# Transposed attention weights in tiles of four heads, one piece per row, two tiles in turn

## The chip, the cores and the metric

The kernel runs on one NeuronCore of a Trainium2 chip. The metric is the device time of one execution in microseconds (us); lower is better. The engines named below are TensorE (PE, matrix products; PEld is its weight load), VectorE (DVE), ScalarE (ACT), GpSimd (POOL) and SyncE (SP), which only issues transfers here. The memories are SBUF, of 128 partitions, PSUM, into which TensorE writes, and the chip's main memory.

## What is computed

One transformer layer on 32 sequences of 100 tokens with 256 features, in float32. A normalized `x` attends to a context of 361 tokens with 16 heads of 64 features; the result is added to `x`. Then comes a feed-forward part with weights and activations rounded to 8 bits, which the change doesn't touch.

```
xn = layernorm(x)                                   # 32 x 100 x 256
Qh, Kh, Vh = xn@WQ, ctx@WK, ctx@WV                  # 16 heads of 64
logits = Qh @ Kh^T / 8 + mask * -1e9                # per head 100 x 361
attn = softmax(logits)
x = x + concat(attn @ Vh) @ WO
x = x + ffn_8bit(layernorm(x))
```

## The kernel before, in words

The 32 sequences ("batches") are worked off one after the other, in groups of four. The first and the last are cut in three parts; the 30 between are "whole" and run through `whole_batch` (L800). For TensorE, VectorE, ScalarE and GpSimd the order of the instructions in that stretch is the order of the Python code; only SP's order is chosen by a scheduler.

A whole batch does its 16 heads in two halves of eight. For each half, TensorE multiplies queries by keys (`products`, L451), one head per PSUM bank. VectorE adds the mask and takes the minimum of each row (`minima`, L465), writing the logits to `pb`, which holds eight heads. ScalarE takes the exponential (L479). TensorE meanwhile makes the keys of the next batch (`k_part`, L285). VectorE divides by the row sums (`divide`, L487 and L494), four heads at a time.

The product with V needs the weights transposed, context tokens on the partitions. The query rows of a head stand in four blocks of 32 partitions, 25 tokens in each. `blocks` (L522) is a VectorE instruction per head that transposes every 32 x 32 block in its place, into the tile `xT`. In it, partition block k still belongs to query block k. `send` (L527) moves the blocks to where they belong with 16 transfers from SBUF to SBUF (L533), issued by SP: for each of four source blocks of 32 partitions and four destination blocks, 32 rows of three pieces (one for each of the three chunks of 128 context tokens) of 200 numbers (eight heads of 25 tokens). There is one `xT` tile for eight heads, with one buffer (`NX` is 1), and one `pT` tile, the destination, for each half.

`attend` (L561) multiplies V by the transposed weights on TensorE. It runs for the batch before: all of batch i-1 stands in TensorE's order after the first half's keys of batch i, and before the second half's `products`. It reads a head's weights from `pT` as four runs of 25 numbers.

After the second half come `residuals`, V of the batch itself (`v_part`, L316; three of its copies on VectorE and three on ScalarE, L324), and once per group of four the queries (`q_part`, L378) and the output projection (`project_T`, L598). SP also issues one load of context per batch (L215), for the batch after the next two; it waits until TensorE has finished with the buffer.

The order around the change, in `whole_batch`:

```
for q in range(half * NQ // 2, (half + 1) * NQ // 2):
    divide(i, range(2 * PAIRS * q, 2 * PAIRS * (q + 1)))
    blocks(i, range(2 * PAIRS * q, 2 * PAIRS * (q + 1)))
send(i, half)
if half == 0:
    attend(i - 1)
```

Of the kernel before, what the change touches and what calls it, by code (L numbers as in the profile page):

```python
# [8 lines left out]
F32 = mybir.dt.float32  # L9
# [18 lines left out]
def kernel(  # L28
# [16 lines left out]
    P = 128  # L45
# [6 lines left out]
    NHP = E // P  # L52
    NFC = F // P
    NSC = 3
    SC = P
    SP = NSC * SC
# [3 lines left out]
    PAIRS = 2  # L60
    NQ = NHP // PAIRS
    HP = NHP // 2
# [5 lines left out]
    QB = 32  # L68
    NQB = P // QB
    TB = T // NQB  # L70
# [97 lines left out]
    with ExitStack() as att:  # L168
        wpool = att.enter_context(tc.tile_pool(name="wpool", bufs=1))
        p1 = att.enter_context(tc.tile_pool(name="p1", bufs=1))  # L170
# [20 lines left out]
        NB = 4 * PAIRS  # L191
        pb = wpool.tile([P, NB, SP], F32, tag="p", name="p")
# [16 lines left out]
        def bank(name):  # L209
            return psum.tile([P, 512], F32, tag="ps", name=name)  # L210
# [28 lines left out]
        for k in range(2):  # L239
            nc.scalar.dma_start(  # L240
                out=maskh[k * RH : k * RH + TH], in_=mask[k * TH : (k + 1) * TH]
            )
        for k in range(NQB):
            nc.scalar.dma_start(
                out=maskt[k * QB : k * QB + TB], in_=mask[k * TB : (k + 1) * TB]
# [18 lines left out]
        steps = []  # L264
# [4 lines left out]
        def whole(i):  # L269
            return steps[i][2] == NHP  # L270
# [131 lines left out]

        pTs, aTs, wides = {}, {}, {}

        def wide(i, half):

            b = steps[i][0]
            if (b, half) not in wides:
                wides[b, half] = p1.tile(
                    [SC, NSC * NQB, NHP * TB], F32, tag=f"pT{half}", name=f"pT{b}_{half}"  # L410
                )
            return wides[b, half]

        def weights_T(i, pair, on_vector):

            h0 = 2 * pair
            pts = [bank(f"pt{i}_{pair}_{k}") for k in range(2)]
            for h in range(2):  # L420
                for c in range(NSC):
                    for k in range(2):
                        ks = slice(k * RH, k * RH + TH)
                        nc.tensor.transpose(
                            pts[k][:SC, (h * NSC + c) * TH : (h * NSC + c + 1) * TH],
                            pb[ks, (h0 + h) % NB, c * SC : (c + 1) * SC],
                            ident[ks, ks],
                        )
            n = 2 * NSC * T
            pT = pTs[i, pair] = wide(i, pair // HP).rearrange("s c t -> s (c t)")[  # L430
                :, pair % HP * n : (pair % HP + 1) * n
            ].rearrange("s (c t) -> s c t", t=T)
            copies = []
            for k in range(2):
                src = pts[k][:SC, : 2 * NSC * TH].rearrange("p (c t) -> p c t", t=TH)
                copy = nc.vector.tensor_copy if k == 0 and on_vector else nc.scalar.copy
                copies.append(copy(pT[:, :, k * TH : (k + 1) * TH], src))
            return copies
# [69 lines left out]

        xTs, NX = {}, 1

        def blocks(i, heads):


            half = heads[0] // NHP
            if (i, half) not in xTs:
                xTs[i, half] = p1.tile(
                    [P, SP // QB, NHP * TB + QB - TB], F32, tag="xT", name=f"xT{i}_{half}", bufs=NX
                )  # L520
            for h in heads:
                nc.vector.transpose(  # L522
                    xTs[i, half][:, :, h % NHP * TB : h % NHP * TB + QB],
                    pb[:, h % NB, :].rearrange("t (c s) -> t c s", s=QB),
                )

        def send(i, half):  # L527

            src = xTs[i, half].rearrange("p (c m) t -> p c m t", c=NSC)
            dst = wide(i, half).rearrange("s (c k) t -> s c k t", c=NSC)  # L530
            for m in range(P // QB):
                for k in range(NQB):
                    nc.sync.dma_start(  # L533
                        out=dst[m * QB : (m + 1) * QB, :, k, :],
                        in_=src[k * QB : (k + 1) * QB, :, m, : NHP * TB],
                    )

        def attend(i, pairs=None):


            b, first, n = steps[i]
            if pairs is not None:
                first, n = pairs
            g, j = b // G, b % G

            def weights(pair, k, c):
                if not whole(i):
                    return pTs[i, pair][:, k * NSC + c, :]
                h = 2 * (pair % HP) + k
                return wide(i, pair // HP)[:, c * NQB : (c + 1) * NQB, h * TB : (h + 1) * TB]  # L550

            if first == 0 and j == 0:
                aTs[g] = p1.tile([P, NHP, G, T], F32, tag="aT", name=f"aT{g}")
            for p0 in range(first, first + n, HP):
                m = min(HP, n)
                av = bank(f"av{i}_{p0}")
                for pair in range(p0, p0 + m):
                    for c in range(NSC):
                        for k in range(2):
                            h = 2 * (pair % HP) + k  # L560
                            nc.tensor.matmul(  # L561
                                av[k * DK : (k + 1) * DK, (pair - p0) * T : (pair - p0 + 1) * T],
                                vs[b, pair // HP][:, c, h * DK : (h + 1) * DK],
                                weights(pair, k, c),
                                start=(c == 0),
                                stop=(c == NSC - 1),
                            )
                copied = nc.scalar.copy(  # L568
                    aTs[g][:, p0 : p0 + m, j, :],
                    av[:, : m * T].rearrange("p (c t) -> p c t", t=T),  # L570
                )
            return copied
# [227 lines left out]
        def whole_batch(i):  # L800

            b = steps[i][0]
            g, j = b // G, b % G
            if not whole(i - 1):
                for pair in range(steps[i - 1][1], steps[i - 1][1] + steps[i - 1][2]):
                    weights_T(i - 1, pair, True)
            if b - 1 + NCB < B:
                load_ctx(b - 1 + NCB)  # L810
            for half in range(2):
                heads = range(half * NHP, (half + 1) * NHP)
                minima(i, products(i, range(half * HP, (half + 1) * HP)))
                n = steps[i + 1][2] // 2
                keys = range(half * n, (half + 1) * n)
                exponentials(i, heads[:6])
                for pair in keys[: n // 2]:
                    k_part(i + 1, pair)
                exponentials(i, heads[6:])
                for pair in keys[n // 2 :]:  # L820
                    k_part(i + 1, pair)
                for q in range(half * NQ // 2, (half + 1) * NQ // 2):
                    divide(i, range(2 * PAIRS * q, 2 * PAIRS * (q + 1)))
                    blocks(i, range(2 * PAIRS * q, 2 * PAIRS * (q + 1)))
                send(i, half)
                if half == 0:
                    attend(i - 1)
            residuals(i, range(2), None)
            if j == G - 2:
                ln1_T(g + 1)  # L830
            v_part(b, 0, 0)
            for piece in todo.pop(0) if todo else ():
                piece()
            for c in range(1, NSC):
                v_part(b, 0, c)
            while later:
                normalize(later.pop(), None)
            for c in range(NSC):
                v_part(b, 1, c)
            if j == G - 3:  # L840
                ln1(g + 1)
            group_work(i, range(2))
            if g == NG - 1 and j >= 1:
                project(b - 1, range(NHP))
# [11 lines left out]
        i = len(steps) - 1  # L856
# [23 lines left out]
    h = hpool.tile([P, NFC, N], F32, tag="h", name="h")  # L880
# [132 lines left out]
    k = 0  # L1013
# [3 lines left out]
    src = xg[0].rearrange("t b d -> t (b d)")  # L1017
# [20 lines left out]
    for u, (g, n) in enumerate(units):  # L1038
# [3 lines left out]
        for fc in range(NFC):  # L1042
# [4 lines left out]
            m = GT // cut  # L1047
            for part in range(cut):
# [16 lines left out]
                if fc + 1 in ends and (u, fc - 1) not in paired:  # L1065
                    src = h[:, fc + 1 - spans[ends.index(fc + 1)] : fc + 1, at if cut > 1 else ts]
# [12 lines left out]
            if (u, fc) in rounded:  # L1079
                i = rounded[u, fc]  # L1080
# [7 lines left out]
            if (u, fc) in ((3, 0), (3, 3)):  # L1088
                p = (2, 4) if fc == 0 else (2, 6)
# [15 lines left out]
    with tc.high_priority():  # L1105
        rh, hih, c2, _, _, found, bounds, product = affine_params(ext2, "h", scales["2"][1])
# [7 lines left out]
    def part(i):  # L1114

        return 2 if blocks[i][1] < 3 or i == len(blocks) - 3 else G
# [18 lines left out]
    for i, (first, n) in enumerate(blocks):  # L1135
# [3 lines left out]
        for k in range(2):  # L1139
            sl = slice(k * NF2, (k + 1) * NF2)  # L1140
            t = f2.tile([P, NF2, G * P], I16, tag=f"ih{k}", name=f"ih{i}_{k}")[:, :, : n * P]
# [16 lines left out]
        m = part(i)  # L1158
# [59 lines left out]
```

## Time and profile before

| what | value |
|---|---|
| median of three runs | 1374.21 us (1372.69 to 1375.06) |
| the profiled execution | 1374.26 us |
| its span, first to last instruction | 1372.5 us |
| PE busy | 1283.0 us (93%) |
| DVE busy | 956.2 us (70%) |
| ACT busy | 583.1 us (42%) |
| mean granted TensorE clock | 0.966 |
| bytes moved by DMA | 106.66 MB, mean 78 GB/s |
| transfers of `send` | 960, of 75.0 KB each, in pieces of 800 bytes |

The span is the time from the first to the last instruction of the profiled execution; the time of the whole execution is 1.8 us longer. Busy time counts computing instructions. The issue of a transfer is not counted as busy; it is listed with the queue that issues it, "SPq" for SP, and its duration is the time that the queue is taken by it. "Landing" is when a transfer's completion is known. An arrow in a wait names what the instruction waited for.

### The profile page before, as it was taken

What the parts mean: (1) busy time and instruction counts of PE and PEld (TensorE: products, weight loads), DVE (VectorE), ACT (ScalarE), POOL (GpSimd) and SP (SyncE); (2) the same over time, 40 slices, a digit from 0 to 9 for tenths busy, and PEclk for the clock granted to TensorE, in tenths of its full rate; (3) what the DMA queues carried; (4) which work ended last, traced back from release to release, by engine and by line L of the source; (5) the groups of instructions that cost most, each with busy time, mean ns of one, the idle gap of its engine ahead of it and who ended that gap; (6) DMA issues with size and microseconds to landing.
All of it is one profiled execution on the core that took longest, in us unless ns stands there. A gap on an engine that the chain in (4) does not pass through costs nothing.

```text
span 1372.5 us, 21080 instructions
## 1 busy us (share of the span) xinstructions
PE 1283.0 (93%) x7186; PEld 743.6 (54%) x7188; DVE 956.2 (70%) x2803; ACT 583.1 (42%) x1570; POOL 111.3 (8%) x195
## 2 busy tenths in 40 slices
PE   9999899889999899899998999899998999998858
PEld 4645556555555565455555555455564555555526
DVE  4666675876577676776757775776668775775798
ACT  2544244433344443342444434344443333442685
POOL 1000000110010100110001100110001100102250
PEclk9999999899998999899998999899999999999998
DMA  8143323323322432333223323323332333221112
GB/s 237 35 109 77 75 59 81 76 72 78 83 69 58 120 75 61 85 85 76 66 66 86 77 68 80 89 63 79 68 77 73 77 83 83 57 62 46 49 54 96
DMA packets 132507, 106.66 MB, mean 78 GB/s; under 512 B 17224, under 2 KB 130448, under 8 KB 132400
## 3 DMA queue, kind: packets, MB, share of 16 engines
q1 hardware_dynamic: 129312, 98.60, 29.6%
q0 software_dynamic: 2144, 5.38, 1.4%
q10 hardware_dynamic: 944, 1.34, 0.3%
q8 instruction: 57, 0.93, 0.3%
q14 instruction: 50, 0.41, 0.1%
HBM read 24.97 MB, written 6.55 MB: 23 GB/s over the span
## 4 chain that ended last, share of the span: by engine, by line
PE 51%; DVE 18%; SPq 17%; DMA 5%; issue 4%; POOL 2%; ACT 2%; DVEq 0%; POOLq 0%
SPq L533 17%; PE pv L316 13%; PE pk L285 12%; DVE xT L522 10%; PE pq L378 6%; PE py L598 5%; DMA pT<-xT 5%; PE av L561 5%; PE sc L451 5%; DVE p L494 3%; PE pf L1164 2%; ACT h L1060 1%; DVE p L465 1%; DVE st L626 1%; POOL r L987 1%
## 5 line engine op out<-in xcount | busy, mean ns | idle before, releaser
L522 DVE STREAM_TRANSPOSE xT<-p 128x384 f32<-128x384 f32 x480 | 277.3, 578 | 238.3 <-DMA pT<-xT 226.0
L479 ACT ACTIVATE p<-p,m 128x361 f32<-128x361 f32 (+1 forms) x512 | 299.0, 587 | 258.4 <-DVE m L465 258.2
L285 PE MATMUL pk<-c,wkt 128*128 128x361 f32 x1016 | 345.1, 495 | 36.1 <-DVE m L465 36.0
L316 PE MATMUL pv<-wvt,c 128*128 128x512 f32 x768 | 336.1, 593 | 0.0
L285 PEld LDWEIGHTS pk<-c,wkt 128*128 128x128 f32 x1016 | 198.3, 200 | 182.5 <-DVE m L465 73.0
L465 DVE CUSTOM_DVE_ANT_0 p<-sc,maskt 128x361 f32<-128x361 f32 x480 | 222.4, 529 | 76.2 <-PE sc L451 76.1
L316 PEld LDWEIGHTS pv<-wvt,c 128*128 128x128 f32 x768 | 144.3, 190 | 170.6 <-issue 166.7
L451 PE MATMUL sc<-kT,q 64*128 64x361 f32 (+1 forms) x1024 | 207.0, 494 | 15.8 <-DVE v L324 7.4
L494 DVE TENSOR_SCALAR p<-p,r 128x361 f32<-128x361 f32 (+1 forms) x512 | 174.6, 405 | 4.4
L324 ACT COPY v<-pv 128x512 f32<-128x512 f32 x90 | 52.8, 586 | 251.5 <-PE pv L316 251.5
L451 PEld LDWEIGHTS sc<-kT,q 64*128 64x128 f32 (+1 forms) x1024 | 102.4, 188 | 103.3 <-DVE v L324 23.3
L561 PE MATMUL av<-pT,v 128*64 128x100 f32 x3072 | 144.9, 252 | 11.2 <-DMA pT<-xT 5.3
L561 PEld LDWEIGHTS av<-pT,v 128*64 128x64 f32 x3072 | 136.2, 137 | 31.0 <-issue 16.2
L292 ACT COPY kT<-pk 128x361 f32<-128x361 f32 x254 | 111.6, 451 | 61.5 <-PE pk L285 61.4
L479 ACT ACTIVATION_READ_ACCUMULATOR p<-p,m 128x1 f32 (+1 forms) x512 | 96.0, 187 | 0.0
L645 POOL TENSOR_SCALAR v<-mv 100x1 f32<-100x1 f32 x31 | 8.4, 272 | 1053.9 <-DVE mv L627 1053.6
L378 PE MATMUL pq<-xnT,wqt 128*128 128x400 f32 x256 | 87.9, 500 | 0.2 <-ACT xnT L369 0.2
L568 ACT COPY aT<-av 128x400 f32<-128x400 f32 (+2 forms) x67 | 31.9, 476 | 107.8 <-PE av L561 107.8
L598 PE MATMUL py<-aT,wot 128*128 128x400 f32 x224 | 76.4, 499 | 0.0
L324 DVE COPY v<-pv 128x512 f32<-128x512 f32 x102 | 65.0, 676 | 9.9 <-PE pv L316 9.8
L378 PEld LDWEIGHTS pq<-xnT,wqt 128*128 128x128 f32 x256 | 48.4, 190 | 38.8 <-issue 3.3
L598 PEld LDWEIGHTS py<-aT,wot 128*128 128x128 f32 x224 | 42.6, 190 | 34.0 <-issue 3.4
(148 smaller groups left out, 692.1 us busy)
## 6 DMA issues: line engine op xcount, KB each, us to landing
pT<-xT SPq DMA_DIRECT2D x960, 75.0 KB
c<-in_ctxT_dram SPq DMA_DIRECT2D x31, 361.0 KB
x<-in_x_dram SPq DMA_DIRECT2D x8, 400.0 KB
xb<-xb POOLq DMA_DIRECT2D x32, 100.0 KB, 2.5
x<-xb SPq DMA_DIRECT2D x5, 384.0 KB
out_dram<-x SPq DMA_DIRECT2D x5, 256.0 KB
out_dram<-x SPq DMA_DIRECT2D x3, 384.0 KB
wqt<-in_wq_dram SPq DMA_DIRECT2D x4, 256.0 KB
```

Source lines behind the costliest of these rows:

```text
L285: nc.tensor.matmul(pk[:, :S], wkt[q][:, dc, col * P : (col + 1) * P], c[:, dc, :S], start=(dc == 0), stop=(dc == NDC - 1),)
L316: nc.tensor.matmul(pv[:SC, :], c[:, dc, s * SC : (s + 1) * SC], wvt[h][:, dc, :], start=(dc == 0), stop=(dc == NDC - 1),)
L324: return copy(vs[b, h][:, s, :], pv[:SC, :])
L378: nc.tensor.matmul(pq[:, :GT], wqt[q][:, dc, pair * P : (pair + 1) * P], xnTs[g][:, dc, :], start=(dc == 0), stop=(dc == NDC - 1),)
L451: nc.tensor.matmul(pss[h], qbuf[pair // PAIRS][k * DK : (k + 1) * DK, pair % PAIRS, b % G, :n], kT[k * DK : (k + 1) * DK, pair, :], start= ...
L465: done = nc.vector.tensor_tensor_reduce(pb[:n, h % NB, :S], ps, maskh if halved(steps[i][0]) else maskt, 1.0, BIG, ALU.add, ALU.min, ms[h] ...
L479: nc.scalar.activation(s, s, AF.Exp, bias=ms[h][:n], scale=-1.0, accum_out=sums[i][0][:n, h : h + 1])
L494: nc.vector.tensor_scalar(s, s, r[:n, h : h + 1], None, ALU.mult)
L522: nc.vector.transpose(xTs[i, half][:, :, h % NHP * TB : h % NHP * TB + QB], pb[:, h % NB, :].rearrange("t (c s) -> t c s", s=QB),)
L533: nc.sync.dma_start(out=dst[m * QB : (m + 1) * QB, :, k, :], in_=src[k * QB : (k + 1) * QB, :, m, : NHP * TB],)
L561: nc.tensor.matmul(av[k * DK : (k + 1) * DK, (pair - p0) * T : (pair - p0 + 1) * T], vs[b, pair // HP][:, c, h * DK : (h + 1) * DK], weigh ...
L598: nc.tensor.matmul(py[:, :GT], wot[:, c, dc * P : (dc + 1) * P], aT[:, c, :, :].rearrange("p j t -> p (j t)"), start=(c == 0), stop=(c == ...
```

## The change

The transposed weights of four heads now have a tile of their own, and two such `xT` tiles are used in turn (`NX` is 2, `NH` is 4 heads). There are four `pT` tiles for a batch, one for each four heads. In both tiles the three chunks of a row stand one behind the other: `RUN` is 4 x 25 + 7 = 107 numbers, of which the last 7 are what a 32-wide block writes beyond its 25, so that a row of one source and one destination block is one piece of 3 x 107 = 321 numbers, 1,284 bytes. `send` is called behind each four heads, with 16 transfers each time, of 32 rows of one piece; in the order of SP's instructions a batch now has 64 of them in place of 32. `blocks` writes its 12 blocks by chunk and destination block, in four dimensions. `attend` reads the same four runs of 25 numbers at other distances, and the parts of the first and last batch that don't use `send` keep their copies in the same, now smaller, tiles.

```
+        NH = 2 * PAIRS
+        RUN = NH * TB + QB - TB
-        def wide(i, half):
+        def wide(i, pair):
-            b = steps[i][0]
-            if (b, half) not in wides:
-                wides[b, half] = p1.tile(
-                    [SC, NSC * NQB, NHP * TB], F32, tag=f"pT{half}", name=f"pT{b}_{half}"
+            b, g = steps[i][0], 2 * pair // NH
+            if (b, g) not in wides:
+                wides[b, g] = p1.tile(
+                    [SC, NQB, NSC * RUN], F32, tag=f"pT{g}", name=f"pT{b}_{g}"
                 )
...
-        xTs, NX = {}, 1
+        xTs, NX = {}, 2
...
-            half = heads[0] // NHP
-            if (i, half) not in xTs:
-                xTs[i, half] = p1.tile(
-                    [P, SP // QB, NHP * TB + QB - TB], F32, tag="xT", name=f"xT{i}_{half}", bufs=NX
+            g = heads[0] // NH
+            if (i, g) not in xTs:
+                xTs[i, g] = p1.tile(
+                    [P, P // QB, NSC, RUN], F32, tag="xT", name=f"xT{i}_{g}", bufs=NX
                 )
             for h in heads:
                 nc.vector.transpose(
-                    xTs[i, half][:, :, h % NHP * TB : h % NHP * TB + QB],
-                    pb[:, h % NB, :].rearrange("t (c s) -> t c s", s=QB),
+                    xTs[i, g][..., h % NH * TB : h % NH * TB + QB].rearrange("p m c s -> p c m s"),
+                    pb[:, h % NB, :].rearrange("t (c m s) -> t c m s", c=NSC, s=QB),
                 )
-        def send(i, half):
-            src = xTs[i, half].rearrange("p (c m) t -> p c m t", c=NSC)
-            dst = wide(i, half).rearrange("s (c k) t -> s c k t", c=NSC)
+        def send(i, g):
             for m in range(P // QB):
                 for k in range(NQB):
                     nc.sync.dma_start(
-                        out=dst[m * QB : (m + 1) * QB, :, k, :],
-                        in_=src[k * QB : (k + 1) * QB, :, m, : NHP * TB],
+                        out=wide(i, g * NH // 2)[m * QB : (m + 1) * QB, k, :],
+                        in_=xTs[i, g][k * QB : (k + 1) * QB, m].rearrange("p c t -> p (c t)"),
                     )
...
-                h = 2 * (pair % HP) + k
-                return wide(i, pair // HP)[:, c * NQB : (c + 1) * NQB, h * TB : (h + 1) * TB]
+                t = c * RUN + (2 * pair + k) % NH * TB
+                return wide(i, pair)[:, :, t : t + TB]
...
                     blocks(i, range(2 * PAIRS * q, 2 * PAIRS * (q + 1)))
-                send(i, half)
+                    send(i, q)
```

More of the change, by code (lines that the diff above doesn't have):

```diff
@@ L403 @@
         pTs, aTs, wides = {}, {}, {}
-        def wide(i, half):
-            b = steps[i][0]
-            if (b, half) not in wides:
-                wides[b, half] = p1.tile(
-                    [SC, NSC * NQB, NHP * TB], F32, tag=f"pT{half}", name=f"pT{b}_{half}"
+        NH = 2 * PAIRS
[5 more added lines that the diff above has]
+                    [SC, NQB, NSC * RUN], F32, tag=f"pT{g}", name=f"pT{b}_{g}"
                 )
-            return wides[b, half]
+            return wides[b, g]
         def weights_T(i, pair, on_vector):
@@ L429, in weights_T @@
             n = 2 * NSC * T
-            pT = pTs[i, pair] = wide(i, pair // HP).rearrange("s c t -> s (c t)")[
-                :, pair % HP * n : (pair % HP + 1) * n
+            pT = pTs[i, pair] = wide(i, pair).rearrange("s k t -> s (k t)")[
+                :, pair % (NH // 2) * n : (pair % (NH // 2) + 1) * n
             ].rearrange("s (c t) -> s c t", t=T)
```

## The prediction, made before the result was known

> **What bounds the kernel now.** I read the chain that ended last first: it says which engines pass the work on.
>
> ```profile
> PE 51%; DVE 18%; SPq 17%; DMA 5%; issue 4%; POOL 2%; ACT 2%; DVEq 0%; POOLq 0%
> SPq L533 17%; PE pv L316 13%; PE pk L285 12%; DVE xT L522 10%; PE pq L378 6%; PE py L598 5%; DMA pT<-xT 5%; PE av L561 5%; PE sc L451 5%; DVE p L494 3%; PE pf L1164 2%; ACT h L1060 1%; DVE p L465 1%; DVE st L626 1%; POOL r L987 1%
> ```
>
> TensorE carries half, but its greatest single line is no computation: SP, issuing the transfers of `send`. The waits say who suffers (total us, times, longest):
>
> ```profile
> DVE xT L522 <- DMA pT<-xT: 226.0, 38, 7.2
> PE av L561 <- DMA pT<-xT: 5.3, 4, 2.5
> SPq L533 <- DVE xT L522: 329.1, 33, 27.7
> ```
>
> VectorE waits for the one `xT` buffer, SP waits longer for VectorE: they take turns. The timeline of one batch:
>
> ```profile
> 505.82 10.22 SPq L533 DMA_DIRECT2D pT<-xT  x16
> 513.09 10.46 PE L316 MATMUL pv<-wvt,c 128*128 128x512 f32 x24
> 517.81 2.42 DVE L522 STREAM_TRANSPOSE xT<-p 128x384 f32<-128x384 f32 x4 [6.20 <-DMA pT<-xT]
> ...
> 521.60 2.41 DVE L522 STREAM_TRANSPOSE xT<-p 128x384 f32<-128x384 f32 x4
> 523.58 0.37 SPq L215 DMA_DIRECT2D c<-in_ctxT_dram  x1
> 524.06 1.23 SPq L533 DMA_DIRECT2D pT<-xT  x2
> ```
>
> Sixteen issues end at 516.0; 1.9 us later VectorE may refill `xT`. TensorE runs on through that wait; it stands still only in some batches, such as the one before, for `pT` and for VectorE:
>
> ```profile
> 460.77 2.29 PE L561 MATMUL av<-pT,v 128*64 128x100 f32 x48 [1.24 <-DMA pT<-xT]
> 462.99 2.70 PE L451 MATMUL sc<-kT,q 64*128 64x361 f32 x16
> 467.44 5.12 PE L285 MATMUL pk<-c,wkt 128*128 128x361 f32 x16 [1.75 <-DVE m L465]
> ```
>
> The stretches (160 us each) from 80 to 1200 us give what TensorE could win at most:
>
> ```profile
> sum 1120.00, PE 1066.35 PEld 612.78 DVE 778.22 ACT 450.06 POOL 66.93; mean PE 152.34 PEld 87.54 DVE 111.17 ACT 64.29 POOL 9.56
> ```
>
> Idle is 160 - 152.3 = 7.7 us per 160. In the timeline the fourth transpose of a batch ends at 67.7 us in the first whole batch and 1209.5 in the thirtieth: (1209.5 - 67.7) / 29 = 39.37 us per batch. SP issues 32 transfers and a load in it.
>
> **The price on which it turns: one issue on SP.** Rows of issues, ns lowest/median/highest:
>
> ```profile
> L533 SPq DMA_DIRECT2D pT<-xT x960: 585/597/2016, 71.7 to 1244.1; - x192
> L215 SPq DMA_DIRECT2D c<-in_ctxT_dram x33: 368/374/421, 0.7 to 1153.2; - x33
> L1132 SPq DMA_DIRECT2D out_dram<-x x11: 351/372/377, 1350.1 to 1369.6; - x11
> L228 SPq DMA_DIRECT2D x<-in_x_dram x8: 413/2166/2539, 2.1 to 28.7; - x8
> L244 ACTq DMA_DIRECT2D maskt<-in_mask_dram x4: 264/264/313, 13.2 to 16.3; - x4
> ```
>
> In the chain these issues follow each other 0.64 us apart (608.05, 608.69): 0.597 and 0.044 between. Now 32 x 0.641 + 0.42 (load) = 20.9 us per batch, half of 39.37. The change issues 64.
>
> Does a third of the pieces make an issue cheaper? Against it: the first of a burst, behind an idle queue, takes 586, so this is no backlog; a 128-row transfer costs 368 with 256 pieces (L222) and with 1,024 (L253), so pieces do not count; one piece per row instead of several saves 15 ns (L1132: 357 against 372). Rows seem to. The completions in the packet list give 5 engines to the 25-row transfer (264), 10 to the 100-row one (413 at its lowest), 16 to the 32-row one (597): 115 + 30 per engine gives 265, 415 and 595, while 128 rows on 16 engines stand apart at 368. So 32 rows of one piece: 597 - 15 = 582, 0.626 us apart, an estimate. Its ends: 351 and 597, L1132's lowest and today's; I take the upper, the same rows, memories and engines.
>
> The Trainium skill, "DMA: Bandwidth & Descriptors", section "Rules for kernel authors", tells to coalesce many small transfers, since under 64 KB one pays mostly overhead. The change goes from 75.0 to 40.1 KB each. By that rule the same bytes cost twice the overhead, 2 x 20.5 = 41 us of issues per batch, more than a batch; by L1132's row it would be 64 x 0.40 = 26.
>
> **Part by part.**
> - Transfers double: 30 x 64 = 1,920. At 0.626, four sends are 4 x 10.02 + 0.42 = 40.5 us per batch of 39.37. This alone makes SP the bound.
> - Pieces: 92,160 of 800 B become 61,440 of 1,284 B (1,200 used, 84 filler). Part 3 gives 129,312 packets 29.6% of 16 engines, 50 ns each; in proportion to bytes at most 84 ns, two per engine and transfer, 0.17 us in 0.626. No bound.
> - Two tiles: the third tile waits only for the first's transfers, so the 6 us stall before it goes. What is late next is the fourth, which waits for the second's, and these stand on SP behind the first's.
> - Sends go out one tile earlier: 3.8 us, once, at the first batch. Within a batch the first send now also waits for `attend`'s first two pairs to have read the `pT` tile: 0.4 us (the timeline gives eight pairs 4.34 us, so two 1.1, begun 0.8 before the tile is full, plus what a semaphore takes). Behind it stand the other sends and the context load, needed two batches later.
> - Transposes (four dimensions instead of three, same 384 columns): 0; L397's four-dimensional copy takes 569 ns for 400 columns, L437's three-dimensional one 464 for 300, no surcharge. `av` reads the same 100 columns in four runs: 0. Both between 0 and, were a run to cost a transpose's excess of 0.18 us over 400 ns, 3 us per batch of VectorE time, covered by its wait for SP.
> - Waits of VectorE: a tile's first transpose stands behind four recorded semaphore waits of 49 ns (236 for 60 tiles), about 0.1 us apart. Two tiles more per batch would be 0.8 us; I cost them at 0, since they pass while the transfer they wait for is still under way. Queued behind them are the tile's division of the next heads and the copies of V, and TensorE waits for both; without that cover the loop grows by these 0.8 us, +24 in all.
>
> The loop, in the order of its waits: a batch's third send begins when the second's issues end. +1.9 landing, +2.4 transposes: the fourth tile is full. From there to the next batch's first full tile the timeline has 14.8 to 19.3 us, typically 16.8 (16.6 where TensorE has least to do: VectorE's own work). +0.4, then two sends until the next third one: 20.0. Sum 1.9 + 2.4 + 16.8 + 0.4 + 20.0 = **41.5 us**, with SP busy for 40.5. (41.5 - 39.37) x 30 = +64, less 3.8: +60. The profiled execution took 1374.26 us (span 1372.5), the median of three is 1374.21: **1434 us**. At 597 ns the period is 42.0: +75, 1449; with SP busy without a gap 40.5: +30, 1404.
>
> **Rivals.**
> - *The issue becomes cheap* (faster, the other side). If pieces or a second dimension make the 597, an issue costs 372, a send 6.7 us, the loop 21.5 + 13.3 = 34.8, below TensorE's busy 152.3/160 x 39.37 = 37.5: TensorE bounds, 30 x (37.5 - 39.37) = -56: 1318. It decides below the issue at which the loop is 39.37: sends of 8.9 us, 0.558 apart, 514 ns. For it: L215, L1132. Against it: the 25-, 100- and 32-row rows on one line.
> - *Half cheap*, 500 to 540 ns: 39 to 40.2 us, -15 to +21: 1359 to 1395; nothing speaks for it but that both layout and count change.
> - *The turn-taking stays, on top*: if each send starts 0.5 us late (waits on VectorE, `attend` and `pT`, with TensorE held in turn by late `pT` tiles), 64 x 0.641 + 0.42 + 2.0 = 43.4: 1491. For it: L533's 61 recorded semaphore waits; against it: with two tiles the next is full before the last one's issues end.
> - *The change doesn't do what it says*: the order of instructions has 16 issues behind each four heads' transposes, so I give it nothing.
>
> **How the numbers follow.** Issue stays (1395 to 1465): 73%; cheap (about 1318): 15%; half cheap: 7%, split 3 faster, 3 same, 1 slower; turn-taking on top: 5%. Slower by over 0.2% (what a measurement of this kernel can tell from no change) 79%, same 3%, faster 18%. The likeliest is 1434; the range 1355 to 1465 leaves out the cheap case and the far end of the slow ones, some 20%.
>
> **What the changed profile would show.** The send's row: 1,920 issues at 575 to 597 ns (price right), or near 370 (wrong, and the time is the rival's). First full tile to first full tile: 41.5 us. SP's wait for VectorE falls from 329 us to some 30; VectorE's idle before the transposes grows past 226; TensorE falls below 93% of the span. Wrong if SP waits for VectorE for hundreds of us again, or if a transpose is over 650 ns.

## The result, and the profile after

The changed kernel takes 1486.47 us (median of four runs, 1482.09 to 1488.82), the kernel before 1374.04: a ratio of 1.0811, 95% interval 1.0795 to 1.0827. It is slower by 112 us. The forecast was slower, at 1434 us, with a range that ended at 1465: the direction was right and the size was not. The profiled execution took 1488.82 us, with a span of 1487.0.

The chain that ended last, the page's part 4:

```profile
PE 50%; SPq 27%; DVE 7%; DMA 6%; issue 4%; ACT 3%; POOL 2%; DVEq 0%; ACTq 0%; POOLq 0%
SPq L535 27%; PE pk L285 16%; PE sc L454 8%; PE pv L316 7%; PE av L563 6%; PE py L600 5%; PE pq L378 5%; DMA pT<-xT 4%; DVE xT L526 3%; ACT h L1062 2%; PE pf L1166 1%; PE po L584 1%; POOL xb L143 1%; DMA wkt<-in_wk_dram 0%; DVE v L324 0%
```

SP's issues rose from 17% to 27% of the chain, in a longer span. Who waits for whom (total us, times, longest):

```profile
DVE xT L526 <- DMA pT<-xT: 322.9, 73, 7.4
PE av L563 <- DMA pT<-xT: 40.4, 15, 6.6
```

```profile
SPq L535 <- DVE xT L526: 28.6, 5, 23.9
```

Before, SP waited 329 us for VectorE and VectorE 226 for SP. Now SP hardly waits (one wait of 23.9 us stands before the first batch), while VectorE's wait has grown, and TensorE, which had waited 5 us for the weights, waits 40. One side of the turn-taking has become the bound. SP's timeline shows it without a sum: start, length, line, count.

```profile
500.60 0.52 SPq L215 DMA_DIRECT2D c<-in_ctxT_dram  x1
501.23 41.30 SPq L535 DMA_DIRECT2D pT<-xT  x64
542.63 0.53 SPq L215 DMA_DIRECT2D c<-in_ctxT_dram  x1
544.19 42.36 SPq L535 DMA_DIRECT2D pT<-xT  x64
```

The 64 issues of a batch stand end to end, 41 to 42 us long; what TensorE has to do in a batch is 35.8 (run 2 below). The row of the issue (lowest, median, highest ns), beside the context load's:

```profile
L535 SPq DMA_DIRECT2D pT<-xT x1920: 507/589/1852, 68.1 to 1359.7; - x192
L215 SPq DMA_DIRECT2D c<-in_ctxT_dram x33: 368/528/1382, 0.7 to 1275.5; - x33
```

The issue costs 589 ns in place of 597. From first full tile to first full tile a batch now takes 43.06 us in place of 39.37. The 29 such periods, 3.69 us longer each, are 107 us of the 114.5 by which the span grew; the other 7 come from the last of these batches and what follows it.

What makes a batch's 43.06 us can be added up from SP's instructions, first send to last (68.1 to 1360.3 us, 1292.2 us for 30 batches): issues 38.68, which is 64 x 0.589 = 37.70 at their median and 0.98 because their average, 604 ns, lies above it; gaps of some 45 ns between instructions, 2.74; loads, 0.57; all longer gaps, SP's waits among them, 1.09. Sum 43.08. SP is taken or between two instructions for 97% of the stretch. The average is pulled up by 53 issues of over 650 ns, which took 1.27 us a batch beyond the median; the short ones, above all the first of a send, took 0.29 less than it.

### The profile page after: what moved, and what is told of

Its sections match the earlier page's. It is cut to its first block, busy times and chain, and to the rows that moved or that the text cites. A ratio compares the mean times of both kernels' runs of the same rounds, so it can differ in the third digit from the quotient of the medians.

```text
span 1487.0 us, 22617 instructions
## 1 busy us (share of the span) xinstructions
PE 1319.8 (89%) x7186; PEld 760.4 (51%) x7188; DVE 962.2 (65%) x2803; ACT 584.0 (39%) x1570; POOL 110.3 (7%) x195
## 3 DMA queue, kind: packets, MB, share of 16 engines
q1 hardware_dynamic: 113952, 103.82, 25.8%
## 4 chain that ended last, share of the span: by engine, by line
PE 50%; SPq 27%; DVE 7%; DMA 6%; issue 4%; ACT 3%; POOL 2%; DVEq 0%; ACTq 0%; POOLq 0%
SPq L535 27%; PE pk L285 16%; PE sc L454 8%; PE pv L316 7%; PE av L563 6%; PE py L600 5%; PE pq L378 5%; DMA pT<-xT 4%; DVE xT L526 3%; ACT h L1062 2%; PE pf L1166 1%; PE po L584 1%; POOL xb L143 1%; DMA wkt<-in_wk_dram 0%; DVE v L324 0%
## 5 line engine op out<-in xcount | busy, mean ns | idle before, releaser
L526 DVE STREAM_TRANSPOSE xT<-p 128x384 f32<-128x384 f32 x480 | 277.7, 579 | 357.9 <-DMA pT<-xT 322.9
L316 PE MATMUL pv<-wvt,c 128*128 128x512 f32 x768 | 340.6, 599 | 12.7 <-DVE rmax L624 12.7
L454 PE MATMUL sc<-kT,q 64*128 64x361 f32 (+1 forms) x1024 | 222.9, 554 | 56.1 <-DVE rmax L624 46.9
L563 PE MATMUL av<-pT,v 128*64 128x100 f32 x3072 | 153.5, 257 | 44.2 <-DMA pT<-xT 40.4
L454 PEld LDWEIGHTS sc<-kT,q 64*128 64x128 f32 (+1 forms) x1024 | 110.3, 214 | 152.6 <-DVE rmax L624 64.8
L563 PEld LDWEIGHTS av<-pT,v 128*64 128x64 f32 x3072 | 142.2, 140 | 65.6 <-issue 36.3
L378 PE MATMUL pq<-xnT,wqt 128*128 128x400 f32 x256 | 92.9, 517 | 10.1 <-DVE v L324 8.6
```

The source lines that it names most:

```text
L316: nc.tensor.matmul(pv[:SC, :], c[:, dc, s * SC : (s + 1) * SC], wvt[h][:, dc, :], start=(dc == 0), stop=(dc == NDC - 1),)
L378: nc.tensor.matmul(pq[:, :GT], wqt[q][:, dc, pair * P : (pair + 1) * P], xnTs[g][:, dc, :], start=(dc == 0), stop=(dc == NDC - 1),)
L454: nc.tensor.matmul(pss[h], qbuf[pair // PAIRS][k * DK : (k + 1) * DK, pair % PAIRS, b % G, :n], kT[k * DK : (k + 1) * DK, pair, :], start= ...
L526: nc.vector.transpose(xTs[i, g][..., h % NH * TB : h % NH * TB + QB].rearrange("p m c s -> p c m s"), pb[:, h % NB, :].rearrange("t (c m s ...
L563: nc.tensor.matmul(av[k * DK : (k + 1) * DK, (pair - p0) * T : (pair - p0 + 1) * T], vs[b, pair // HP][:, c, h * DK : (h + 1) * DK], weigh ...
```

## The experiments

All are compared with the kernel before, run on the same chip. Where a ratio is given it has its 95% interval.

**1. The price of an issue by rows.** The tile of four heads goes out straight, in transfers of many sizes, so the weights land in the wrong places; a single execution.

```
for k, p, n in ((0, 0, 128), (1, 0, 64), (1, 64, 32), (1, 96, 16), (1, 112, 8), (1, 120, 8),
                (2, 0, 100), (2, 100, 25), (2, 125, 3), (3, 0, 96)):
    nc.sync.dma_start(out=pT[p : p + n, k, :], in_=xT[p : p + n, k]...)   # one piece per row
nc.sync.dma_start(out=pT[96:, 3]..., in_=xT[96:, 3]...)                   # 32 rows, three pieces
```

> The changed kernel, but each tile of four heads goes out in 11 straight transfers of different row counts (partition p to partition p), so the weights land in the wrong places. What is read is the duration of an issue on SP by its shape, one piece of 1,284 bytes per row: 128, 64, 32, 16, 8, 8, 100, 25, 3 and 96 rows, and 32 rows of three pieces of 400 bytes. Theory A (the price is set by rows and engines, 115 + 30 ns per engine unless there are 128 rows): 128 rows 370, 64, 32, 16 and 96 rows about 590, 8 rows 355, 100 rows 415, 25 rows 265, 3 rows 205, and 32 rows in three pieces 597. Rival B (the price is that of a copy from SBUF to SBUF): 128 rows cost about 590 like 32. Rival C (pieces): 32 rows in three pieces cost clearly more than 32 in one, and 128 rows more than 64.

Medians of 120 issues each: 128 rows 531 ns (always the first of a burst), 64 rows 599, 32 rows 593, 16 rows 589, 96 rows 557; 8 rows 724 and 656, 100 rows 789, 25 rows 727, 3 rows 685; 32 rows in three pieces 687, here right behind the 96-row one. Theory A of the prices, 115 + 30 ns per engine, is refuted: 25 rows, which it put at 265, cost 727, and 128 rows are no cheap exception. Row counts that are a multiple of 16 cost much the same, 531 to 599 ns. C has one row for it, whose neighbour differs; run 6 puts the pieces' price at 8 ns.

**2. The same bytes in four transfers.**

```
for m in range(P // QB):
    nc.sync.dma_start(out=pT[:, m, :], in_=xT[:, m].rearrange("p c t -> p (c t)"))
```

> The changed kernel with 4 transfers of 128 rows per tile in place of 16 of 32 rows; same bytes, same tiles and waits, and the blocks aren't exchanged between partitions, so the weights land in the wrong places. If SP's issues are the bound (theory A), 16 issues per batch free SP and TensorE bounds: 1290 to 1330 us. If the waits of the two tiles, of landing and of the four destination tiles make the loss (rival), they are all still there: above 1400 us.

1258.15 us in a single execution. The tiles, their waits and the bytes are all there; the number of issues has gone from 64 to 16 a batch, and the loss with it. The transfers have 128 rows each and leave out the exchange between partitions. The rival, that the waits alone make the loss, is refuted. The issue of 128 rows from SBUF to SBUF:

```profile
L535 SPq DMA_DIRECT2D pT<-xT x480: 464/600/1557, 67.3 to 1122.8; - x160
```

It costs 600 ns, as 32 rows do (464 at its lowest, behind an idle queue). TensorE is busy for 97% of the span, for 99.5% of the stretch from 80 to 1040 us, and its mean granted clock is 0.995; a batch takes 35.82 us. That is what TensorE needs when it hardly ever stands still.

**3. The layout alone.** Tiles of eight heads, one of them, one piece per row.

```
-        NH = 2 * PAIRS
+        NH = 4 * PAIRS
-        xTs, NX = {}, 2
+        xTs, NX = {}, 1
-                    send(i, q)
+                send(i, half)
```

> The layout alone: one piece per row (2,484 bytes), but tiles of eight heads, one of them, sent behind eight heads as before: 32 transfers per batch. Theory A (a piece costs 8 ns of an issue's 597): 32 x 0.008 = 0.26 us per batch at most, 1366 to 1375 us, the same or faster by up to 0.6%. If the layout itself (1,284-byte steps for TensorE's reads, transposes in four dimensions, filler bytes) makes the loss: above 1400.

1374.33 us, ratio 0.9992 (0.9978 to 1.0005): no change. The issue's median is 589 ns here as well:

```profile
L535 SPq DMA_DIRECT2D pT<-xT x960: 507/589/2052, 71.7 to 1243.7; - x192
```

Longer pieces, filler, four dimensions in the transposes and the other distances in TensorE's reads cost nothing that can be measured, and gain nothing while 32 issues a batch leave SP idle half of the time.

**4. Half of the issues on GpSimd.**

```
-                    nc.sync.dma_start(
+                    queue = nc.gpsimd if k % 2 else nc.sync
+                    queue.dma_start(
```

> The changed kernel with every second transfer of a tile issued by GpSimd in place of SP, nothing left out: 32 issues per batch on each. Theory A (SP's issues are the bound): a tile is out in 8 x 0.63 = 5 us on SP and 8 x 0.7 = 5.6 on GpSimd, the loop of 43 us falls below TensorE's own work, 1290 to 1340 us, faster than both kernels. Rival (the waits of landing, destination tiles and VectorE make the loss): 1440 or more.

1327.17 us, ratio 0.9652 (0.961 to 0.9693): faster than both kernels, with nothing left out. A row for each queue:

```profile
L536 SPq DMA_DIRECT2D pT<-xT x960: 507/588/2204, 67.3 to 1185.0; - x192
L536 POOL DMA_DIRECT2D pT<-xT x960: 496/498/892, 67.9 to 1186.1; - x192
```

SP's price is the same and GpSimd's is lower. VectorE's wait for the transfers falls from 322.9 us to 5.6; another one has come:

```profile
DVE x L150 <- POOL xb L143: 67.2, 14, 7.7
```

GpSimd's additions for the residual stand behind the fourth tile's issues in its order, and VectorE waits for them.

**5. The kernel before, with half of the issues on GpSimd** (the same edit in its `send`).

> The kernel before (one tile of eight heads, three pieces per row) with every second transfer issued by GpSimd. A tile is out in some 5 us in place of 10.2, so VectorE's 6 us waits shrink to about 1.5. If the issue rate is all that counts (theory A), it comes to 1315 to 1340 us, as the changed kernel with the same split did (1327). If the two tiles in turn are worth something of their own once the issues are cheap (theory A2), it stays above 1340, and the difference to 1327 is their worth.

1368.42 us, ratio 0.9941 (0.9924 to 0.9958). By the expectation that spoke for two tiles; but VectorE waits 67.8 us for GpSimd's additions here too, so the run doesn't separate the two. Run 9 does.

**6. Three pieces per row again, in the changed kernel.**

```
-                        in_=xTs[i, g][k * QB : (k + 1) * QB, m].rearrange("p c t -> p (c t)"),
+                        in_=xTs[i, g][k * QB : (k + 1) * QB, m, :, : NH * TB],
```

> The changed kernel (two tiles of four heads, 64 transfers per batch), but with three pieces of 400 bytes per row in place of one of 1,284: the one-piece layout alone undone. Theory A (SP's issues are the period, 597 ns with three pieces, 589 with one): 64 x 0.008 = 0.5 us per batch, 30 batches, +15 us against the changed kernel: 1495 to 1508 us. Rival (the waits are the period, SP has room): no difference, 1480 to 1492.

1504.74 us, ratio 1.0923 (1.0887 to 1.096), 18 us more than the changed kernel. The kernel before was 2.6 us slower beside this run than beside the changed kernel; by the two ratios the difference is 15 us. The row of the issue:

```profile
L536 SPq DMA_DIRECT2D pT<-xT x1920: 585/597/2004, 68.2 to 1374.6; - x192
```

Eight nanoseconds on 1,920 issues are 15 us, and about as much comes. Here SP has no room: what an issue costs more is paid. In run 3 the same eight were worth nothing.

**7. The same 32 rows from main memory.** Four of a tile's 16 transfers read rows of WQ.

```
+                    if m == 0:
+                        here = wq[k * QB : (k + 1) * QB, : NSC * RUN]
```

> The changed kernel, but 4 of the 16 transfers of a tile (those for the first 32 destination partitions) read 32 rows of 1,284 bytes of WQ from main memory in place of the tile, so those weights are wrong. Same rows, same pieces, same destination; only the memory of the source differs. If the rows set the price of an issue (theory A of the prices): about 590 ns, like the other twelve. If a copy from SBUF to SBUF is what costs (theory B): 360 to 430 ns, like the context load and the output.

```profile
L538 SPq DMA_DIRECT2D pT<-xT x1440: 507/589/1848, 68.3 to 1302.6; - x180
L538 SPq DMA_DIRECT2D pT<-in_wq_dram x480: 310/419/1882, 33.6 to 1294.6; - x160
```

419 against 589 ns, with equal rows, pieces and destination, and 310 against 507 at their lowest. Theory B holds for the source: reading from SBUF in place of main memory is what makes the issue dear, by 170 ns. The destination was SBUF in both. The whole took 1432.14 us in a single execution: a quarter of 64 issues cheaper by 0.17 is 2.7 us a batch, 82 in all, and 54 came. By the trace SP's issues became 2.5 us a batch shorter, but the short gaps between its instructions grew from 2.74 to 3.20 us and the longer ones from 1.09 to 1.30, which leaves 1.9.

**8. The fourth tile on SP alone.**

```
+                    queue = nc.gpsimd if k % 2 and g < 3 else nc.sync
```

> The changed kernel with every second transfer of the first three tiles of a batch issued by GpSimd, and the fourth tile wholly by SP: 24 on GpSimd, 40 on SP. In the run with half of all on GpSimd, VectorE waited 67 us for GpSimd's additions for the residual, which stand in GpSimd's order behind the fourth tile's issues. If that wait is on the path: it goes, and 1300 to 1320 us. If SP's longer fourth send is what counts (40 x 0.63 + 0.4 = 26 us per batch, but 10 us at the batch's end): 1327 to 1345.

1278.10 us, ratio 0.9288 (0.9264 to 0.9313), better than expected. VectorE waits 16.6 us for GpSimd's additions in place of 67.2:

```profile
DVE x L150 <- POOL xb L143: 16.6, 13, 3.4
```

TensorE is busy for 97%, its granted clock is 0.991, a batch takes 36.26 us: 0.4 above run 2's.

**9. The kernel before, its first half split and its second half on SP.**

```
+                    queue = nc.gpsimd if k % 2 and half == 0 else nc.sync
```

> The kernel before with every second transfer of the first half's tile issued by GpSimd and the second half's tile wholly by SP: 8 on GpSimd and 24 on SP per batch. With half of all on GpSimd (1368) the additions for the residual stood behind the second half's issues; here they do not. If that order alone kept the old layout from gaining, this comes to 1290 to 1320 us and two tiles are worth little beyond (1278 for the changed kernel split in the same way). If the tiles are what counts, 1335 to 1365.

1309.74 us, ratio 0.952 (0.9501 to 0.9539). The wait for GpSimd's additions is gone (14.0 us), VectorE still waits 115.8 for its one tile. So most of what the old layout could gain is in the rate of issues and in GpSimd's order. Two tiles of four, split in the like way (run 8), are another 32 us lower.

**10. One tile of four heads, issues split as in run 8** (`NX` is 1).

> The changed kernel split between SP and GpSimd as in the run of 1278 us (fourth tile on SP alone), but with one buffer for the four-head tiles in place of two. Each tile's transposes now wait for the send before: 5 us of issues and 2 of landing, against 1.4 us of division between them. If the second tile is worth something: the wait comes four times a batch, +2 to +4 us per batch, 1340 to 1400. If cheap issues alone make the gain: 1275 to 1290.

1594.05 us, ratio 1.1585 (1.1554 to 1.1616), slower than expected.

```profile
DVE xT L526 <- DMA pT<-xT: 426.5, 93, 8.8
```

Each tile now waits out the send of the one before: 46.87 us per batch against 36.26, 2.7 us for each of four tiles. If tiles are halved, there must be two.

**11. The fourth tile split too, behind the additions.**

```
-                    send(i, q)
+                    if q < NQ - 1:
+                        send(i, q)
...
             residuals(i, range(2), None)
+            send(i, NQ - 1)
```

> The changed kernel with half of every tile's transfers on GpSimd, but the fourth tile's are issued behind the additions for the residual in GpSimd's order (in the run of 1327 us they stood before them, in that of 1278 the fourth tile was SP's alone). If the order on GpSimd made those 49 us, this is 1270 to 1285. If SP's longer fourth send helped in some other way: 1310 or more.

1276.92 us, ratio 0.9282 (0.9261 to 0.9304). Against run 4 only the place of the fourth send in the program differs; VectorE's wait for the additions is 16.2 us in place of 67.2, and the time 50 lower.

```profile
DVE x L150 <- POOL xb L143: 16.2, 13, 3.1
```

So that order made the 49 us between runs 4 and 8. This is the fastest version here that computes everything, equal to run 8 within their spread, and 14% below the changed kernel.

**12. Twelve issues a batch on GpSimd, 52 on SP** (`k == 3 and g < 3`).

> The changed kernel with a quarter of the first three tiles' transfers on GpSimd, the fourth tile SP's alone: 52 issues on SP per batch, 12 on GpSimd; between 64 (1486 us) and 40 (1278 us). Two theories of what sets the period once SP has room. Loop (landing 1.9, transposes 2.4, 16.8 to the next batch's first full tile, 0.4, then the fourth tile's send of 16 x 0.634 and the first one's of 12 x 0.634): 39.2 us per batch, 1365 to 1385. Sum of SP's issues (52 x 0.634, 1.0 of long issues, 0.6 of load, 1 of waits = 35.6, below TensorE's 36): TensorE bounds, 1278 to 1310.

1346.95 us, ratio 0.9792 (0.9772 to 0.9811), 38.54 us per batch. The loop had said 39.2, the sum of the issues 35.6 with TensorE's 36 above it. Neither time was met, but the loop's is nearer: VectorE waits 142.5 us for transfers while SP stands idle for 126 of its 1,153, so it is not the sum of the issues that sets the period. The loop is 0.7 us too long, 20 us in 30 batches.

## Why the prediction was right or wrong, point by point

- *SP becomes the bound*: right. Runs 2, 4, 8, 11 and 12 take issues from SP, by different means, and the time falls each time; run 6 makes them dearer, and it rises. Run 10 takes issues from SP as well, but leaves a single tile, and waits for that.
- *Pieces do not count, bytes are no bound, layout costs nothing*: right for an issue in a row (run 3). The DMA engines' share of the send's queue fell from 29.6% to 25.8%.
- *An issue costs 582 ns*: nearly right at the median, 589. The reason, a line through the engines used, was wrong: run 1 refutes the line, and run 7 shows that the source in SBUF counts. That the destination counts too is only suggested, by the output's row (SBUF to main memory, 351 to 377 ns). The forecast's reason fitted three rows taken on two queues with different sources; no row of the kernel before let the source alone change. One piece saved 8 ns in a row, not the 15 of the output's rows, and the forecast's "no backlog" does not hold for it: behind an idle queue such an issue takes 507 ns (585 with three pieces), so 82 of the 589 belong to its place in the row.
- *The loop of 41.5 us*: this is the step that failed. SP became the bound, as forecast, but the price of its issues, the term on which the sum turns, was mis-sized: the period is longer by 1.6 us a batch, 47 us of the 52 by which the forecast missed. I put every issue at 582 ns, an estimated median; the 1,920 issues average 604. Of the 1.6 us, 0.45 is the median, 7 ns higher; 0.98 is the average, 15 ns above the median, because of 53 long issues (up to 1.85 us); 0.15 is the load, which cost 528 ns behind a full queue and not 374; the rest cancels. The kernel before showed a longest issue of 2,016 ns, and its 960 issues average 614 ns, 17 above their median. With SP idle half of the time this had cost little, and I left it out; 17 ns on 64 issues are 1.1 us a batch. All this is a sum of recorded durations; no run took the long issues away.
- *Idle of about 1 us a batch on SP*: 1.09 on average, but not by the forecast's steady loop, in which SP waits in every batch. In 18 of 29 cases SP went from one batch's last send to the next one's first with at most the load between. Term by term the loop was, on average, 2.4 us from the first full tile to its send (0.4 in the forecast), 21.1 for two sends (20.0), 4.0 to the fourth full tile (4.3) and 15.6 to the next first one (16.8): the first tile often stands full before a busy SP. That the idle time came out right is partly luck.
- *What the two tiles shift* came as said: the third tile is full on average 11.4 us after the second (14.7 before), and the fourth, which now waits for the second's transfers, 10.3 us after the third (3.9 before). The other signs came too: VectorE's wait for the transfers grew to 322.9 us, TensorE's busy share fell to 89%, and SP's wait for VectorE fell to 28.6 us.
- *The estimate from the rule to coalesce*, 41 us of issues a batch, came close: 41.4 with the gaps. The price of an issue hardly moved when its bytes were nearly halved.
- *The rivals*: a cheap issue did not come. The price of turn-taking on top, 1491, lies near the result, but not by its mechanism: SP's longer gaps are 1.1 us a batch, where that rival has 2.0 of late sends, and the rest is in the issues. TensorE is held by late weights, as it said, for 40 us in all.
- *TensorE's bound of 1318* for a cheap issue was too high: 1258 (run 2). I took its busy time, 37.5 us a batch, as fixed. In run 2 it is 35.6. In those stretches the granted clock rose from 0.97 to 1.00, which accounts for 1.1 us of the 1.9; the rest was not traced.

## What to carry to other kernels

Before a transfer is cut into more and smaller ones, count its issues times the issue's price and set them against the period of the stage; here 64 x 0.634 = 40.6 us stood against 39.4. An issue's price is read for the same pair of memories and for issues in a row, and as an average with its rare long cases, since a saturated queue pays for all of them. Finer tiles are worth having once a second queue shares the issues, and the order on that queue must not put them before work that another engine waits for.

## What the runs showed of the hardware that was not expected

**SP's long issues coincide with instruction loading.** In the changed kernel 53 issues took over 650 ns, mostly 1.0 to 1.8 us. A packet of an instruction queue (q8 or q14 in the profile's list of queues, 16 and 8 KB) starts within each of the 53, or at most 0.75 us ahead; by that measure only 176 of all 1,920 issues have one near. Before, it was 24 of 26: twice the issues, twice the long ones. That these packets cause the delay is read from the coincidence; no run took them away.

**Part of an issue's duration belongs to what stands ahead of it.** An issue of 32 rows in one piece takes 507 ns behind an idle queue and 589 behind its like; of 128 rows, 464 and 600 (rows of runs 2 and 3). In run 7 an issue that reads SBUF takes 513 ns behind one that reads main memory, and the latter 524 behind one that reads SBUF, 419 behind its like. The context load's 374 ns became 528 in the changed kernel in the same way. So a price read from the first issue of a burst is too low for those behind it. What the queue waits for there, no run shows.

**A direct copy in a row is cheaper to issue on GpSimd**: 498 ns against SP's 588 in run 4, where SP's lowest is 507. The Trainium skill, "DMA: Bandwidth & Descriptors", section "Issuing engines are not separate DMA queues", says that issuing from several engines saves only the sequencer's time, usually small beside the transfer. The mechanism agrees: the transfers and their bytes stayed the same. The size does not: here that time was the bound, and sharing it took the changed kernel from 1486 to 1277 us.

**TensorE's clock falls behind a stall.** TensorE stands still for 3.0 us in the changed kernel, finishes `attend`, and does the `products` of eight heads, here beside those of a later stretch without a stall:

```profile
501.88 2.27 PE L563 MATMUL av<-pT,v 128*64 128x100 f32 x24 [3.00 <-DMA pT<-xT]
504.08 4.68 PE L454 MATMUL sc<-kT,q 64*128 64x361 f32 x16
...
535.20 2.70 PE L454 MATMUL sc<-kT,q 64*128 64x361 f32 x16
```

The stretch of the slow `products` and the one that follows; columns are the stretch, its length, the busy times of PE, PEld, DVE, ACT and POOL, the granted clock, the DMA share and GB/s:

```profile
504.00:508.70 4.70, 4.70 (x19) 2.55 (x17) 2.94 (x12) 2.93 (x10) 0.00 (x0) 0.56 0.25 65
```

```profile
508.70:523.00 14.30, 14.30 (x40) 7.32 (x39) 6.48 (x20) 5.28 (x15) 0.00 (x0) 1.00 0.24 64
```

At a clock of 0.56 they take 4.68 us in place of 2.70; in the 2.2 us of `attend` before them it is 0.50. So the clock is low for some 6 us of work behind a stall of 3.0, and the stall costs more than its length. Over the whole kernel the granted clock is 0.931, before 0.966, in run 2 0.995. The Trainium skill, "TensorE: Matmul & The Clock Gate", section "Part 1: The HAM clock gate", has the clock at half after an idle window of about 3.4 us and full again after about as long of work; the row agrees in kind, but here the stall was 3.0 us and the slow work behind it longer than the page's time.

**Row counts that are no multiple of 16 cost more to issue**: in run 1, 100 rows 789 ns, 25 rows 727, 8 rows 656 and 724, 3 rows 685, against 557 to 599 for 96, 64, 32 and 16 rows. By the forecast's count of engines these are the transfers on fewer than 16, which it had put as cheaper. Why is open; neighbours in the queue differ, too.
